# A two-layer graph attention kernel: one-hots and node loads moved to the end of a step, links ahead of most edge features, chunk 0 last in the sums, x read from the input

## The chip, the cores and the metric

The kernel runs on one core of a Trainium2 chip. The core has five engines that work side by side and wait for one another through semaphores: PE (TensorE, matmuls and transposes), DVE (VectorE), ACT (ScalarE), POOL (GpSimd) and SP (SyncE, which here only issues DMA transfers). The metric is the device time of one execution in microseconds (us); lower is better.

## The reference

A graph of N = 6250 nodes with D = 256 features and E = 200,000 edges, sorted by destination. The input is normalized, goes through two attention layers (4 heads of 64, then one head of 256), and is added back at the end. Cut to one layer:

```python
te = relu(edge_attr @ We + be) * exp(x @ Wo + bo)[src][:, None]        # 64 features of an edge
src, dst, ea = add_self_loops(src, dst, te, n)                         # a loop: mean of te over a node's edges
hx = (x @ Wg).reshape(n, heads, f)
he = (ea @ Wge).reshape(-1, heads, f)
al = leaky_relu((hx*a_s).sum(-1)[src] + (hx*a_d).sum(-1)[dst] + (he*a_e).sum(-1), 0.2)
al = exp(al - segment_max(al, dst)[dst])
al = al / segment_sum(al, dst)[dst]
out = segment_sum(hx[src] * al[:, :, None], dst) + b
x = relu(out + x)      # layer 0; layer 1: out + x + (the normalized input) + (the input)
```

So for every edge a row of its source node is fetched from a table, weighted by a softmax over the edges of its destination, and added up by destination.

## The kernel before

**Tables and steps.** The kernel first normalizes the nodes, multiplies them by the weights of layer 0 and writes table T0 to DRAM (this is the prologue). One row of T0 holds the 268 numbers that an edge needs (the 256 features of `hx`, and terms of the scores) and beside them, in the second half of a row of 2 x 268, a copy of x of that node. Since a gather sees the table as rows of 268, the source indices in `self.src` are doubled. T1, the table of layer 1, has the same two halves and is written during layer 0.

The 200,000 edges, padded, are 1563 chunks of 128 edges. A step handles 24 chunks (the last two of a layer 14 and 13), so that a layer has 66 steps; its destinations lie within a stretch of 112 nodes. In `edges()` one loop runs over the steps `st` of both layers, with work for the next step `nx` and the finished ones `pv` and `late` woven in. The order in which `edges()` calls its parts is the order on each engine's queue; nothing reorders it.

**A step, in the order of `edges()`:**
- `nodes` (SP): the node tile `tw` of a step two ahead, 112 rows of the table with x beside them, in one DMA. `load_lb`, `load_ea`, `load_fl` (SP): other inputs of later steps.
- `gather(nx)` (POOL, L846): 24 indirect DMAs, one for each chunk of 128 rows, into one of three G buffers. A batch can begin once the sums that read this buffer three steps earlier are complete.
- `logits(st)` (DVE, L1043 to L1060): scores of the edges and two scans for the maxima; `ends(st)` (PE, L1067): transposes what the scans leave at the edges of the chunks.
- `spread(nx)` (DVE, L964 and L965, in every second step, for two steps): one-hots of destinations that bring node terms to edges; `parts(nx)` (DVE L993 to L996, PE L1001): the node terms split into bf16 parts.
- `rphase1(nx)` (PE L935, ACT L940): edge features of the next step in two rounds, each of two halves of the columns (four matmul instructions) and one ReLU. It is a generator: `next(y)` runs one round and `drain(y)` the rest.
- `links(st)` (DVE scans L1077 and L1079, PE transpose L1084): maxima across chunk borders, with the previous step's last state.
- `rows2(late)` (PE L452, for the next layer's table), `maxima(st)` (DVE from L1094, ACT), `rphase2(nx)` (PE L949), `adst(nx)` (PE L1015), `scale(st)` (DVE L1148: one operation over all 24 chunks of G).
- `carried(st)` (DVE L1133 to L1138 in layer 0, L1130 and L1138 in layer 1): adds the previous step's unfinished last row into chunk 0 of G.
- `sums(st)` (PE L1160): the one-hot S of a chunk times its G, 48 matmul instructions for 24 chunks, all into one PSUM tile `u`.
- `edge_rows(nx)` (DVE L1029 and L1032), `onehots(nx)` (DVE L980), `finish(pv)` (outputs and rows of finished nodes), `evict(st)` (ACT L1165: `u` to U), `rows1(pv)` (PE L1253), `index_on` (DVE and others: the index work for later steps, in pieces).

`ending()` is a version of the same order for the last steps of a layer.

**The prologue** runs over groups of seven node tiles: statistics, normalization, transposes, matmuls, and `store(g)`, which writes a group's rows to T0. `keep_x(g)` copies x from an input `xt` to the second half of the rows of T0, from DRAM to DRAM (L350). Beside it runs `indices()`, which loads `src` (`self.src`) and doubles it in four operations of 392 columns (L478).

Where the order of the loop decides, these are the lines:

```python
self.gather(nx)
drain(self.logits(st))
self.ends(st)
self.spread(nx)
self.parts(nx)
y = self.rphase1(nx)
next(y)
self.links(st)
...
drain(self.scale(st))
self.carried(st)
self.sums(st)
```

Of the kernel before, what the change touches and what calls it, by code (L numbers as in the profile page):

```python
# [22 lines left out]
F32 = mybir.dt.float32  # L23
BF = mybir.dt.bfloat16
I32 = mybir.dt.int32
# [6 lines left out]
P = 128  # L32
# [47 lines left out]
class Kernel:  # L80
# [122 lines left out]
    def prologue(self):  # L203
# [7 lines left out]
        with ExitStack() as c:  # L211
# [33 lines left out]
            if NT * P < N + P:  # L245
                nc.sync.dma_start(self.T[0][NT * P:N + P, :], zero[:N + P - NT * P, :2 * L.TW])
            trows = [wp.tile([P, GT, L.TW], F32, name=f"trow{i}", bufs=1) for i in range(3)]
# [103 lines left out]

# [19 lines left out]
            for k in range(-3, len(tiles) + 1):  # L371
# [10 lines left out]
                if k == 5:  # L382
                    more()
                if k >= 8 and k % 4 == 0 and k // 4 - 2 < g0:
                    keep_x(k // 4 - 2)
                if 0 <= k + 1 < len(tiles):
# [71 lines left out]
    def indices(self, wp):  # L458
# [16 lines left out]
        yield  # L475
        for i in range(0, NCH, 392):
            src = self.src[:, i:min(NCH, i + 392)]
            V.tensor_scalar(src, src, 2.0, None, op0=OP.mult)  # L478
            yield
        scf = wp.tile([P, 11, NS], F32, name="scf", bufs=1)  # L480
# [168 lines left out]
    def edges(self, ctx):  # L649
# [30 lines left out]
        for k, st in enumerate(steps):  # L680
# [21 lines left out]
            next(y)  # L702
            self.links(st)
            if late:
                self.rows2(late)
# [10 lines left out]
            self.carried(st)  # L716
            self.sums(st)
            if late:
# [25 lines left out]
    def ending(self, st, nx, pv, late, after):  # L744
# [12 lines left out]
        y = self.rphase1(nx)  # L757
        next(y)
        self.links(st)
        if late:  # L760
# [20 lines left out]
        self.evict(st)  # L781
        y = self.rphase1(after) if after else iter(())
        next(y, None)
        drain(self.scale(nx, cuts=(1, 1 + c // 2, c)))
# [54 lines left out]
    def gather(self, st):  # L839
# [5 lines left out]
        for c in (range(0) if st["k"] == 0 and self.CX > last else (last, *range(last))):  # L845
            nc.gpsimd.indirect_dma_start(  # L846
                out=G[:, c, 0:L.TW], out_offset=None, in_=self.rows[L.l][0:2 * n, :],
                in_offset=bass.IndirectOffsetOnAxis(ap=idx[:, c:c + 1], axis=0))
# [56 lines left out]
    def nodes(self, st):  # L905
# [3 lines left out]
        st["tw"], st["xw"] = tw[:, :L.TW], tw[:, L.TW:L.TW + D]  # L909
        w = L.TW + D  # L910
        nc.sync.dma_start(tw[1:M + 1, :w], self.T[L.l][ds(r, M), 0:w])

    def halves(self, st):
# [5 lines left out]
    def rphase1(self, st):  # L919
# [11 lines left out]
        for i in range(2):  # L931
            r = slice(i * PH, (i + 1) * PH)
            y = self.ps_y.tile([P, 1024], F32, name="y")
            for w, o in self.halves(st):
                nc.tensor.matmul(y[:, o], self.webd[l][r, :], ea[r, w], start=True, stop=True)  # L935
            if c % 2:
                for w, o in self.halves(st):
# [125 lines left out]

    def ends(self, st):

        e = st["ends"]
# [256 lines left out]
    def general_layer(self, L, wp, pp):  # L1323
# [13 lines left out]
        with tc.For_i(0, self.NCH * P, P) as i:  # L1337
# [11 lines left out]
            old = wp.tile([P, L.W], F32, name=f"gold{l}")  # L1349
            sw, dw = [wp.tile([P, 1], I32, name=n) for n in ("gsi2", "gdi2")]  # L1350
            V.tensor_scalar(sw, si, 2.0, None, op0=OP.mult)
            V.tensor_scalar(dw, di, 2.0, None, op0=OP.mult)
            for t, tab, ix in ((G[:, :L.TW], self.rows[l], sw), (nd, self.rows[l], dw), (old, state, di)):
# [94 lines left out]
def layout(inputs):  # L1448
# [5 lines left out]
    a = {"x": np.concatenate([x, np.zeros((2 * P, D), np.float32)])}  # L1454
    a["xt"] = np.concatenate([a["x"], np.zeros((N + 2 * P, Layer(0).TW - D), np.float32)], 1)
    EP = NCH * P
# [63 lines left out]
```

## Time and profile before

| | us |
|---|---|
| median of 3 runs (lowest to highest) | 4721.76 (4721.40 to 4724.88) |
| the profiled execution | 4717.79 |
| its span | 4716.0 |
| busy: PE | 3204.3 (68%) |
| busy: POOL | 3015.5 (64%) |
| busy: DVE | 2842.0 (60%) |
| busy: ACT | 524.2 (11%) |
| first gather from T0 | 105.61 |

The profile shows one execution on the chip. In it a row of a group reads: line of the kernel, engine, operation, output<-inputs with their shapes, count | busy time and mean ns of one | idle time of the engine just before them, and what ended most of it. A row of the timeline reads: start, duration, engine, line, operation, and in brackets the idle time before it and what released it. "issue" is time in which the engine waited for nothing that the profile shows; "remote" is a release that it can't name by an instruction. A row of the windows gives busy time and instructions of each engine in a stretch of time, then the clock granted to PE, the DMA engines' mean busy share and GB/s. Shares over the whole span mix the prologue, two layers with different work and the passage between them, so a change in one stage is read from that stage.

### The profile page before, as it was taken

What the parts mean: (1) busy time and instruction counts of PE and PEld (TensorE: products, weight loads), DVE (VectorE), ACT (ScalarE), POOL (GpSimd) and SP (SyncE); (2) the same over time, 40 slices, a digit from 0 to 9 for tenths busy, and PEclk for the clock granted to TensorE, in tenths of its full rate; (3) what the DMA queues carried; (4) which work ended last, traced back from release to release, by engine and by line L of the source; (5) the groups of instructions that cost most, each with busy time, mean ns of one, the idle gap of its engine ahead of it and who ended that gap; (6) DMA issues with size and microseconds to landing.
All of it is one profiled execution on the core that took longest, in us unless ns stands there. A gap on an engine that the chain in (4) does not pass through costs nothing. (4 is left out here: it accounts for less than half of the span.)

```text
span 4716.0 us, 33666 instructions
## 1 busy us (share of the span) xinstructions
PE 3204.3 (68%) x9878; PEld 1931.3 (41%) x9878; DVE 2842.0 (60%) x6122; ACT 524.2 (11%) x1162; POOL 3015.5 (64%) x3255
## 2 busy tenths in 40 slices
PE   7677677776777777777755666666666666666666
PEld 5344444444444444444433334343433333343434
DVE  6566676666676666666664555555545555554546
ACT  4111111111111111111110000000000000000000
POOL 5566666666666666666636666666666666666664
PEclk8767767767777777676676777776777777776777
DMA  8344444444444444444434444444444444444442
GB/s 275 94 128 128 117 126 131 119 127 128 116 127 129 125 122 126 127 121 126 122 84 113 120 118 127 116 123 121 124 117 122 127 121 119 119 125 114 122 124 74
DMA packets 234171, 582.99 MB, mean 124 GB/s; under 512 B 62185, under 2 KB 84613, under 8 KB 233913
## 3 DMA queue, kind: packets, MB, share of 16 engines
q0 software_dynamic: 150144, 422.75, 34.1%
q1 hardware_dynamic: 83419, 157.36, 10.1%
q8 instruction: 79, 1.29, 0.1%
q14 instruction: 113, 0.93, 0.1%
q10 hardware_dynamic: 416, 0.67, 0.1%
HBM read 549.44 MB, written 37.92 MB: 125 GB/s over the span
## 5 line engine op out<-in xcount | busy, mean ns | idle before, releaser
L846 POOL DMA_INDIRECT G<-T,src x3102 | 2962.0, 955 | 1623.1 <-issue 898.9
L1160 PE MATMUL u<-G,S 128*128 128x270 f32 (+1 forms) x6252 | 1621.4, 411 | 750.2 <-issue 628.7
L1160 PEld LDWEIGHTS u<-G,S 128*128 128x128 f32 x6252 | 1235.8, 200 | 1075.8 <-issue 682.0
L935 PE MATMUL y<-ea,webd 64*128 64x384 f32 (+1 forms) x1056 | 734.8, 822 | 304.5 <-issue 269.2
L1148 DVE TENSOR_TENSOR G<-G,kps 128x6144 f32<-128x6144 f32 (+3 forms) x136 | 853.0, 6275 | 0.0
L1077 DVE TENSOR_TENSOR_SCAN cl<-fl,cl,lf 4x129 f32<-4x129 f32 (+1 forms) x130 | 61.2, 471 | 937.2 <-remote 657.0
L935 PEld LDWEIGHTS y<-ea,webd 64*128 64x128 f32 x1056 | 290.2, 298 | 597.1 <-issue 534.7
L949 PE MATMUL zad<-R,wea 128*64 128x384 f32 (+1 forms) x1056 | 464.3, 794 | 2.3 <-ACT R L940 1.0
L980 DVE TENSOR_TENSOR S<-kps,loc 128x3072 f32<-128x3072 f32 x132 | 437.6, 3315 | 4.5
L940 ACT ACTIVATE R<-y,webd 128x768 f32<-128x768 f32 x260 | 233.1, 897 | 627.6 <-PE y L935 272.3
L949 PEld LDWEIGHTS zad<-R,wea 128*64 128x64 f32 x1056 | 155.9, 202 | 314.1 <-issue 253.5
L1165 ACT ACTIVATE U<-u 128x270 f32<-128x270 f32 (+1 forms) x132 | 51.9, 393 | 1880.4 <-remote 913.1
L1029 DVE STREAM_TRANSPOSE rt<-zad 128x768 f32<-128x768 f32 (+1 forms) x130 | 124.5, 958 | 35.2 <-remote 27.8
L1067 PE MATMUL lf<-ident,fb 128*36 128x128 f32 (+1 forms) x132 | 47.1, 357 | 138.2 <-issue 108.7
L1001 PE MATMUL zad<-a,Q 128*128 128x12 bf16 (+1 forms) x132 | 24.4, 185 | 156.6 <-issue 98.5
L452 PE MATMUL fin<-wg,h1T 128*128 128x260 f32 x264 | 127.2, 632 | 1.8 <-ACT h1T L1255 1.8
L1094 DVE TENSOR_TENSOR fb<-flpen,lf 128x192 f32<-128x192 bf16 (+1 forms) x132 | 36.7, 278 | 148.2 <-PE lf L1084 128.6
L964 DVE TENSOR_TENSOR lb<-lb,kps 128x1536 bf16<-128x1536 bf16 (+1 forms) x68 | 113.0, 1661 | 0.0
L452 PE MATMUL ps<-wg,hT 128*128 128x266 f32 x292 | 89.9, 436 | 33.3 <-ACT hT L326 14.9
L452 PEld LDWEIGHTS fin<-wg,h1T 128*128 128x128 f32 x264 | 71.5, 299 | 48.5 <-issue 34.6
L1001 PEld LDWEIGHTS <-Q 128*128 128x128 bf16 x132 | 14.9, 113 | 180.2 <-issue 104.4
L1190 ACT ACTIVATE mw<-mw,mg 128x2 f32<-128x2 f32 x66 | 19.7, 298 | 608.0 <-DVE mg L1189 337.1
(191 smaller groups left out, 2079.4 us busy)
## 6 DMA issues: line engine op xcount, KB each, us to landing
G<-T,src POOLq DMA_INDIRECT x3102
ea<-in_ea_dram SPq DMA_DIRECT2D x64, 768.0 KB
lb<-locrow SPq DMA_DIRECT2D x64, 384.0 KB
tw<-T SPq DMA_DIRECT2D x66, 229.2 KB
T<-t1row SPq DMA_DIRECT2D x66, 227.5 KB
tw<-T SPq DMA_DIRECT2D x66, 225.8 KB
out_dram<-fb SPq DMA_DIRECT2D x64, 112.0 KB
T<-in_xt_dram SPq DMA_DIRECT2D x5, 938.0 KB
```

The lines of the kernel that those rows point to most:

```text
L452: self.nc.tensor.matmul(ps[:, :L.MW], hT[:, k, :], self.wg[L.l][:, k, :], start=(k == 0), stop=(k == 1))
L846: nc.gpsimd.indirect_dma_start(out=G[:, c, 0:L.TW], out_offset=None, in_=self.rows[L.l][0:2 * n, :], in_offset=bass.IndirectOffsetOnAxis(a ...
L935: nc.tensor.matmul(y[:, o], self.webd[l][r, :], ea[r, w], start=True, stop=True)
L940: nc.scalar.activation(R[:, i, :32 * c].rearrange("p (b n) -> p b n", b=2), y.rearrange("p (b n) -> p b n", b=2)[:, :, :16 * c], AF.Relu, ...
L949: nc.tensor.matmul(st["zad"][i * PH:(i + 1) * PH, o], self.wea[l][0], R[:, i, w], start=True, stop=False)
L964: V.tensor_tensor(lb[:, :, :n], lb[:, :, :n], self.k_part.unsqueeze(2).to_broadcast([P, i, n]), op=OP.is_equal)
L980: nc.vector.tensor_tensor(st["S"][:, c0:c1, :], self.k_iota.unsqueeze(1).to_broadcast(w), self.loc[:, o + c0:o + c1].unsqueeze(2).to_broad ...
L1029: V.transpose(rv[:, :32 * c].rearrange("p (b n) -> p b n", b=2), z.rearrange("p (b n) -> p b n", b=2)[:, :, :16 * c])
L1077: V.tensor_tensor_scan(cl[:H, :], fl[:H, :], lf[:H, 0:P + 1], init, op0=OP.add, op1=OP.max)
L1148: nc.vector.tensor_tensor(v, v, pw[:, c0:c1, :].unsqueeze(3) .to_broadcast([P, c1 - c0, H, L.F]), op=OP.mult)
L1160: nc.tensor.matmul(st["u"][:, :L.W], S[:, i, :], G[:, i, 0:L.W], start=(j == 0), stop=(j == c - 1))
L1165: self.nc.scalar.activation(U[:, :L.W], st["u"][:, :L.W], AF.Copy)
```

## The change

- Table T0 loses its second half: its rows are 268 wide, `keep_x` and the input `xt` are gone, and the gather of layer 0 uses rows without doubling. `store` writes whole rows.
- `self.src` is no longer doubled in the prologue, since layer 0 uses it as it is. Layer 1's table keeps two halves, so each step of layer 0 doubles its own 24 columns in `ends()`, after its gathers have used them.
- `nodes` of layer 0 loads `tw` in two DMAs: 112 x 268 from T0 and 112 x 256 from the input x. Layer 1 still uses one.
- `nodes` for three steps ahead stands at the end of a step. On SP's queue this is where the call at the head of the next step stood.
- `spread` for two steps ahead stands at the end of a step, after `index_on`: on DVE ahead of the next step's logits, and no longer behind them. The call `spread(nx)` in its old place then finds the work done.
- `rphase1` can pause after the first half of a round as well. With one `next(y)` before `links(st)` and one after, the transpose of the links (PE) stands after two of the eight L935 matmul instructions, and no longer after four.
- `sums` takes chunks 1 to 23 first and chunk 0, the only one that `carried` writes to, last.

```diff
-        self.T = [self.dp.tile([N + P, L.TW * 2], F32, name=f"T{L.l}") for L in self.L]
+        self.T = [self.dp.tile([N + P, L.TW * (1 + L.l)], F32, name=f"T{L.l}") for L in self.L]
...
-                nc.sync.dma_start(self.T[0][0:NT * P, :].rearrange("(p t) d -> p t d", p=P)
-                                  [:, ts[0]:ts[0] + n, 0:L.TW], trow[:, :n, :])
-
-            def keep_x(g):
-                ts, n = groups[g], len(groups[g])
-                to, of = (t.rearrange("(p t) d -> p t d", p=P)[:, ts[0]:ts[0] + n, :]
-                          for t in (self.T[0][0:NT * P, L.TW:2 * L.TW], a["xt"][0:NT * P, :]))
-                nc.sync.dma_start(to, of)
+                nc.sync.dma_start(self.T[0][0:NT * P, :].rearrange("(p t) d -> p t d", p=P)[:, ts[0]:ts[0] + n, :],
+                                  trow[:, :n, :])
...
-        for i in range(0, NCH, 392):
-            src = self.src[:, i:min(NCH, i + 392)]
-            V.tensor_scalar(src, src, 2.0, None, op0=OP.mult)
-            yield
...
             y = self.rphase1(nx)
             next(y)
             self.links(st)
+            next(y)
...
             self.carried(st)
-            self.sums(st)
+            self.sums(st, (1, st["C"]), (0, 1))
...
                 next(self.late, None)
+            for q in steps[k + 3:k + 4]:
+                if q["L"] is st["L"]:
+                    self.nodes(q)
+            for q in steps[k + 2:k + 3]:
+                if q["L"] is st["L"] and "lb" in q:
+                    self.spread(q)
...
-                out=G[:, c, 0:L.TW], out_offset=None, in_=self.rows[L.l][0:2 * n, :],
+                out=G[:, c, 0:L.TW], out_offset=None, in_=self.rows[L.l][0:n * (1 + L.l), :],
...
-        w = L.TW + D
+        w = L.TW + L.l * D
         nc.sync.dma_start(tw[1:M + 1, :w], self.T[L.l][ds(r, M), 0:w])
+        if L.l == 0:
+            nc.sync.dma_start(st["xw"][1:M + 1, :], self.a["x"][ds(r, M), :])
...
                 nc.tensor.matmul(y[:, o], self.webd[l][r, :], ea[r, w], start=True, stop=True)
+                if o.start == 0:
+                    yield
...
     def ends(self, st):
+        if st["L"].l == 0:
+            src = self.src[:, st["o"]:st["o"] + st["C"]]
+            self.nc.vector.tensor_scalar(src, src, 2.0, None, op0=OP.mult)
```

More of the change, by code (lines that the diff above doesn't have):

```diff
@@ L245, in prologue @@
             if NT * P < N + P:
-                nc.sync.dma_start(self.T[0][NT * P:N + P, :], zero[:N + P - NT * P, :2 * L.TW])
+                nc.sync.dma_start(self.T[0][NT * P:N + P, :], zero[:N + P - NT * P, :L.TW])
             trows = [wp.tile([P, GT, L.TW], F32, name=f"trow{i}", bufs=1) for i in range(3)]
@@ L383, in prologue @@
                     more()
-                if k >= 8 and k % 4 == 0 and k // 4 - 2 < g0:
-                    keep_x(k // 4 - 2)
                 if 0 <= k + 1 < len(tiles):
@@ L757, in ending @@
         y = self.rphase1(nx)
+        next(y)
         next(y)
@@ L782, in ending @@
         y = self.rphase1(after) if after else iter(())
+        next(y, None)
         next(y, None)
@@ L1349, in general_layer @@
             old = wp.tile([P, L.W], F32, name=f"gold{l}")
-            sw, dw = [wp.tile([P, 1], I32, name=n) for n in ("gsi2", "gdi2")]
-            V.tensor_scalar(sw, si, 2.0, None, op0=OP.mult)
-            V.tensor_scalar(dw, di, 2.0, None, op0=OP.mult)
+            sw, dw = [wp.tile([P, 1], I32, name=n) for n in ("gsi2", "gdi2")] if l else (si, di)
+            if l:
+                V.tensor_scalar(sw, si, 2.0, None, op0=OP.mult)
+                V.tensor_scalar(dw, di, 2.0, None, op0=OP.mult)
             for t, tab, ix in ((G[:, :L.TW], self.rows[l], sw), (nd, self.rows[l], dw), (old, state, di)):
@@ L1454, in layout @@
     a = {"x": np.concatenate([x, np.zeros((2 * P, D), np.float32)])}
-    a["xt"] = np.concatenate([a["x"], np.zeros((N + 2 * P, Layer(0).TW - D), np.float32)], 1)
     EP = NCH * P
```

## The prediction

> **What bounds the kernel now.** I read the page's costliest groups first, then busy time by windows around a step in the middle of each layer, then POOL and PE in order of time there, and the prologue last. The groups:
>
> ```profile
> span 4716.0 us, 33666 instructions
> L846 POOL DMA_INDIRECT G<-T,src x3102 | 2962.0, 955 | 1623.1 <-issue 898.9
> ```
>
> No engine is full, but POOL's 3102 gathers are busy 2962 us and idle 1623 us before them, together 4585 of the 4716 us. Inside a batch the idle time is issue (899 us, 0.30 us each); the rest lies between batches. Around one layer-0 step, in windows:
>
> ```profile
> 1218.00:1232.00 14.00, 13.03 (x28) 5.47 (x26) 11.39 (x18) 3.01 (x6) 10.40 (x11) 0.55 0.51 153
> 1232.00:1242.00 10.00, 9.38 (x40) 7.68 (x41) 8.91 (x24) 0.91 (x3) 7.58 (x8) 1.00 0.48 132
> 1242.00:1254.00 12.00, 3.98 (x9) 2.25 (x9) 4.75 (x13) 0.42 (x1) 4.99 (x6) 0.60 0.33 94
> ```
>
> (Columns: length, busy time and count of PE, weight loads, DVE, ACT, POOL; then granted clock, DMA share, GB/s.) A step has three thirds: a chain of edge features at half clock, sums at full clock, and 12 us in which PE and DVE do little. In order of time, POOL and PE:
>
> ```profile
> 1218.53 0.94 POOL L846 DMA_INDIRECT G<-T,src  x1 [5.89 <-PE u L1160]
> ...
> 1247.57 0.95 POOL L846 DMA_INDIRECT G<-T,src  x1 [0.30 <-issue]
> 1254.47 0.94 POOL L846 DMA_INDIRECT G<-T,src  x1 [5.95 <-PE u L1160]
> ...
> 1232.16 9.38 PE L1160 MATMUL u<-G,S 128*128 128x270 f32 x40 [0.83 <-issue]
> 1242.44 0.39 PE L1160 MATMUL u<-G,S 128*128 128x270 f32 x1 [0.90 <-issue]
> ...
> 1250.14 0.61 PE L1160 MATMUL u<-G,S 128*128 128x270 f32 x1 [1.49 <-issue]
> 1252.24 1.96 PE L1160 MATMUL u<-G,S 128*128 128x270 f32 x4 [1.49 <-issue]
> ```
>
> Twenty-four gathers take 1218.53 to 1248.52, 30.0 us. The next batch needs the G buffer that these sums read, so it waits for the last of the 48 matmuls and starts 35.94 us after the batch before. Forty matmuls take 9.4 us, but four single ones take the next 10 us ("issue": nothing the profile shows holds them). This stall lifts near 1252, some 3.7 us after the last gather, and four matmuls follow in 1.96 us, 0.49 us each. So a layer-0 step costs what the stall leaves of the sums. Layer 1:
>
> ```profile
> 3214.00:3228.00 14.00, 2.49 (x7) 1.40 (x7) 1.17 (x6) 0.00 (x0) 7.65 (x9) 0.61 0.36 102
> 3228.00:3239.00 11.00, 9.54 (x19) 3.56 (x18) 9.11 (x12) 2.39 (x4) 8.16 (x9) 0.56 0.34 90
> 3228.40 0.94 POOL L846 DMA_INDIRECT G<-T,src  x1 [4.31 <-remote]
> 3228.16 0.39 ACT L1165 ACTIVATE U<-u 128x261 f32<-128x261 f32 x1 [18.64 <-remote]
> ```
>
> Here the sums are nearly done when the stall comes, and POOL still restarts only when it lifts: a floor that does not move with the sums. Step lengths, from evictions of u (the first and last of 50 layer-0 steps, then of 58 layer-1 steps):
>
> ```profile
> 475.93 0.40 ACT L1165 ACTIVATE U<-u 128x270 f32<-128x270 f32 x1 [12.82 <-PE fin L1253]
> 2237.95 0.40 ACT L1165 ACTIVATE U<-u 128x270 f32<-128x270 f32 x1 [10.92 <-PE u L1160]
> 2612.48 0.39 ACT L1165 ACTIVATE U<-u 128x261 f32<-128x261 f32 x1 [18.61 <-PE zad L1001]
> 4597.30 0.39 ACT L1165 ACTIVATE U<-u 128x261 f32<-128x261 f32 x1 [18.64 <-remote]
> ```
>
> 1762.0/50 = 35.24 us in layer 0 and 1984.8/58 = 34.22 in layer 1. Layer 0 stands 1.0 us a step above the floor: that is all the steps can give, 62 us over its 61 or so full steps.
>
> **The change, part by part.**
>
> *Prologue: x no longer copied into table 0, indices no longer doubled there.*
>
> ```profile
> 40.00:60.00 20.00, 12.03 (x54) 9.50 (x55) 14.06 (x59) 7.56 (x20) 7.95 (x26) 0.83 1.06 330
> 60.00:80.00 20.00, 20.00 (x109) 16.66 (x108) 16.00 (x65) 16.18 (x43) 15.29 (x55) 1.00 1.06 310
> DMA packets 5969, 9.11 MB, mean 304 GB/s; under 512 B 783, under 2 KB 5132, under 8 KB 5900
> T<-in_xt_dram SPq DMA_DIRECT2D x5, 938.0 KB
> T<-in_xt_dram SPq DMA_DIRECT2D x2, 670.0 KB
> T<-in_xt_dram SPq DMA_DIRECT2D x2, 268.0 KB
> 45.19 0.36 DVE L478 TENSOR_SCALAR src<-src 128x392 int32<-128x392 int32 x1 [11.14 <-DMA src<-in_src_dram]
> ```
>
> Nine copies go, 5 x 938 + 2 x 670 + 2 x 268 = 6566 KB. Between 30 and 60 us the DMA engines move 304 GB/s, so this is 21.6 us of all of them. (The Trainium skill, "DMA: Bandwidth & Descriptors", section "Where 436 GB/s comes from", puts the engines' limit at 436 GB/s; by it the copies would be 15.1 us, an estimate; the trace's 304 decides here.) The doubling also loses DVE's 11.14 us wait, though the next index operations wait for a load of their own. Neither is gained whole: PE is full from 60 to 80, and idle 8 us from 40 to 60. I take 8 us; ends 0 (PE's work sets the end) and 20. The first steps' gathers then start earlier, into the stall already shown, which is why I stay low.
>
> *Doubling 24 chunks' indices at each layer-0 step*: one DVE operation more, queued ahead of the boundary transpose. The nearest row is a 128x24 operation (first below):
>
> ```profile
> 3231.28 0.18 DVE L1102 TENSOR_TENSOR mt<-al,m 128x24 f32<-128x24 f32 x1
> 104.89 2.15 SPq L911 DMA_DIRECT2D tw<-T  x3
> ```
>
> 0.2 us x 64 = 13 us at most; it usually falls into the stall, where DVE waits anyway: 0, ends 0 and +13. *Node tile in two DMAs*: SP spends 0.72 us on an issue (second row), 64 more. Behind it on SP's queue stand loads for later steps; the tile is asked for three steps ahead, some 105 us: 0. No row shows what one more issue does to the stall: −0 to +0.3 us a step by the 0.28 us that I find below for half a matmul left over; I take 0. POOL loses a DVE wait on the indices at no cost, since its first gather waits for PE.
>
> *Links after half of the first edge features, chunk 0 last* (layer 0):
>
> ```profile
> 1222.04 0.26 PE L1084 MATMUL lf<-ident,cl 36*128 36x36 f32 x1
> 1222.34 0.35 DVE L1094 TENSOR_TENSOR fb<-flpen,lf 128x192 f32<-128x192 bf16 x1 [1.79 <-PE lf L1084]
> 1224.58 6.54 DVE L1148 TENSOR_TENSOR G<-G,kps 128x6144 f32<-128x6144 f32 x1
> 1231.90 0.21 DVE L1138 SCALAR_TENSOR_TENSOR G<-U,slink,G 1x5 f32<-1x5 f32 x1
> 1230.83 0.50 PE L1015 MATMUL zad<-lb,aq 128*128 128x384 bf16 x2
> ```
>
> Two L935 matmuls, 0.73 us each by the 2.92 us for four (below, under layer 1), go behind the links transpose: it comes up to 1.4 us earlier, and so does the 6.54 us scaling. PE's own chain gets no shorter; its end at 1231.33 is what remains once chunk 0 no longer waits for the carried rows (to 1232.11). The sums start 0.8 us earlier. Whether the stall moves too isn't shown; if it stays, 0.8/0.23 = 3.5 matmuls more lie before it and 3.5 x 0.49 is over the whole 1.0; if it moves along, nothing is gained. I take 0.25 us x 46 steps = −11.5, ends 0 and −46.
>
> *One-hots of destinations at the end of a step.* The index work of every fourth step delays the logits, and with the two one-hot operations behind them the next step starts so:
>
> ```profile
> 1182.36 0.40 ACT L1165 ACTIVATE U<-u 128x270 f32<-128x270 f32 x1 [12.05 <-PE u L1160]
> 1182.79 1.73 DVE L964 TENSOR_TENSOR lb<-lb,kps 128x1536 bf16<-128x1536 bf16 x1
> 1185.66 0.19 PE L1001 MATMUL zad<-a,Q 128*128 128x12 bf16 x1 [2.33 <-DVE a L996]
> 1188.50 0.26 PE L1084 MATMUL lf<-ident,cl 36*128 36x36 f32 x1
> ```
>
> PE waits 2.33 us for parts that stand behind them on DVE, and the links come 6.1 us after the eviction. POOL's next batch starts at 1218.53, 36.17 us after this eviction; a batch follows its own eviction by 0.24 (3228.16 and 3228.40), so this step takes 35.9, 1.7 above the floor. With the pair ahead of the logits some of its 1.73 + 0.4 us falls into the stall; the logits are then late next, by no more than the pair. I take two thirds of the 1.7, −1.1 x 15 = −16.5; ends +5 (the logits late by 0.3) and −33 (the whole pair).
>
> *Layer 1.* The links wait for scans that the stall holds, and half of the edge features now stands behind that wait, at half clock:
>
> ```profile
> 3227.88 2.72 PE L935 MATMUL y<-ea,webd 64*128 64x384 f32 x4 [1.23 <-issue]
> 3231.65 2.92 PE L935 MATMUL y<-ea,webd 64*128 64x384 f32 x4 [0.99 <-ACT R L940]
> ```
>
> Here it costs PE up to 0.7 us; where all four ran in the stall, up to 1.4. The floor covers it: ACT waits 18.64 us for a u that is nearly complete when the stall begins, so the sums have several us of room. Without the cover it is 64 x 0.7 = 45 us. I take +1, ends −5 and +45. (The Trainium skill, "TensorE: Matmul & The Clock Gate", Part 1 on the clock gate, lets 3.4 us of work restore the clock, which would halve that price. The trace differs: from 1218 to 1232 PE is busy 13.03 of 14 us at 0.55.)
>
> **Sum.** −8 − 11.5 − 16.5 + 1 = −35. The profiled execution took 4717.79 us, which gives 4682.8; the median of the runs is 4.0 above it: 4687.
>
> **The rivals.**
> *A. Layer 0 falls to the floor.* For it: layer 1's steps and the shape of the stall, which ends with the gathers. Against: the stall is in every step and may come earlier with the work. 62 + 8 = −70: 4652.
> *B. The stall moves with the sums, and only the prologue counts.* For it: in layer 1, with sums that start earlier, the stall starts earlier too (near 3214, 14 us before the release, against 12 at 1242). −8 or nothing: 4714 to 4722.
> *C. Slower: the stall overtakes the sums of layer 0.* If it begins after so much work is issued, and the earlier links and doubled indices issue more before it, matmuls are left over at the release, each 0.49 us. From 0.27 matmuls a step (8/61/0.49) the prologue's gain is gone; at 1.5 it is 45 − 8 = +37: 4759. Against: layer 0's PE and DVE work per step hardly grows.
>
> **How the numbers follow.** 0.2% is 9.4 us, about what a measurement tells from no change. Forecast (4665 to 4712) 0.42, A 0.18, B 0.15, C 0.25. Faster is forecast and A, 0.60; same is B, 0.15; slower is C, 0.25. The range goes from A's 4645 to 4748, over half of C, and leaves out about 0.2.
>
> **What would show it.** Right: no copies into T from in_xt; the 60 to 80 us stretch without idle PE coming sooner, and the first table gather some 8 us sooner; layer-0 steps near 34.8; the links about 1.3 us sooner after the eviction in steps like 1218, and 2 us or more sooner in those like 1182; sums starting about 0.8 us sooner; layer 1 at 34.2. Wrong: a layer-0 step at or above 35.2 with more than four matmuls after the release (B, C), or layer-1 evictions more than 34.3 us apart.

## The result: 4756.72 us against 4722.64, and the profile after

| | before | after |
|---|---|---|
| median (lowest to highest), us | 4722.64 (4721.40 to 4726.35) | 4756.72 (4748.47 to 4759.31) |
| ratio of after to before | | 1.0067 (95% interval 1.0057 to 1.0077) |
| profiled execution's span, us | 4716.0 | 4755.3 |
| first eviction of u (prologue and first step), us | 192.4 | 179.3 |
| a step of layer 0, mean of 50, us | 35.24 | 35.82 |
| passage between the layers (eviction 60 to 66), us | 237.1 | 233.4 |
| a step of layer 1, mean of 58, us | 34.22 | 34.53 |

The change made the kernel 0.7% slower. The table adds up: the prologue gave 13.1 us, some 60 full steps of layer 0 took 0.58 x 60 = 35 more, the passage gave 4, and some 60 steps of layer 1 took 0.31 x 60 = 19 more: +37, against 39 between the spans. An execution more than 1.5% above the fastest of its kernel, which is taken to be in a slower state, is left out of every comparison; this concerns three of the four executions of run 10.

The page of the changed kernel has the same shape. POOL's gathers are busy 16 us less than before, and idle 65 us longer:

```profile
span 4755.3 us, 34012 instructions
L843 POOL DMA_INDIRECT G<-T,src x3102 | 2945.7, 950 | 1687.7 <-issue 904.9
```

The step lengths come from the same four evictions as before (the first and the last of 50 steps, then of 58):

```profile
467.90 0.40 ACT L1170 ACTIVATE U<-u 128x270 f32<-128x270 f32 x1 [10.69 <-PE u L1165]
2259.14 0.40 ACT L1170 ACTIVATE U<-u 128x270 f32<-128x270 f32 x1 [12.51 <-PE lf L1072]
2633.30 0.39 ACT L1170 ACTIVATE U<-u 128x261 f32<-128x261 f32 x1 [18.12 <-PE u L1165]
4636.24 0.39 ACT L1170 ACTIVATE U<-u 128x261 f32<-128x261 f32 x1 [17.86 <-PE u L1165]
```

The prologue did what was forecast, and more. In windows, and POOL's first gathers from the table:

```profile
40.00:60.00 20.00, 20.00 (x108) 16.39 (x107) 19.07 (x83) 15.94 (x40) 13.05 (x47) 1.00 0.90 327
60.00:80.00 20.00, 20.00 (x109) 16.75 (x108) 16.52 (x75) 15.72 (x42) 11.72 (x37) 1.00 0.75 217
89.78 0.94 POOL L843 DMA_INDIRECT G<-T,src  x1 [14.61 <-DMA T<-trow]
```

PE is busy from 40 us on, where it idled 8 of 20 us before, the DMA share falls from 1.06 to 0.75 in the second stretch, and the first gather starts at 89.78 instead of 105.61.

Now a layer-0 step, PE and POOL in order of time, that stands for most (36.1 us):

```profile
1257.31 0.94 POOL L843 DMA_INDIRECT G<-T,src  x1 [4.68 <-PE lf L1072]
1258.99 0.26 PE L1089 MATMUL lf<-ident,cl 36*128 36x36 f32 x1
1269.32 0.82 PE L1016 MATMUL zad<-lb,aq 128*128 128x384 bf16 x2
1269.93 9.43 PE L1165 MATMUL u<-G,S 128*128 128x270 f32 x39
1280.51 0.39 PE L1165 MATMUL u<-G,S 128*128 128x270 f32 x1 [1.14 <-issue]
1282.61 0.39 PE L1165 MATMUL u<-G,S 128*128 128x270 f32 x1 [1.72 <-issue]
1285.42 0.61 PE L1165 MATMUL u<-G,S 128*128 128x270 f32 x1 [2.42 <-issue]
1288.22 0.61 PE L1165 MATMUL u<-G,S 128*128 128x270 f32 x1 [2.19 <-issue]
1290.31 2.87 PE L1165 MATMUL u<-G,S 128*128 128x270 f32 x5 [1.48 <-issue]
1293.46 0.94 POOL L843 DMA_INDIRECT G<-T,src  x1 [6.46 <-PE u L1165]
```

The links come 1.7 us after the restart of POOL's batch (3.5 us in the step shown of before), the sums 12.6 us after it (13.6), with no wait for the carried rows. But the stall comes sooner too: its first single matmul is at 1280.5, 23.2 us after the restart, where it was 23.9. Thirty-nine matmuls lie before it instead of forty, and five follow the release instead of four. The means below take the stall to begin where PE first stands idle for more than 1 us behind the tenth matmul of the sums; the matmuls that it finds left are those of the 48 that start after that. Over layer 0's full steps in each trace, counted from the eviction, the sums start at 14.07 us before and 12.74 after, the stall begins at 24.8 and 23.0, and it finds 5.4 and 6.9 matmuls left.

Two kinds of steps lie under these means, and the clock granted to PE tells them apart. The step behind the one shown is of the other kind. First the windows at the head of the two steps (the granted clock is the third number from the end), then rows of PE in the second:

```profile
1257.00:1268.00 11.00, 10.57 (x21) 4.84 (x22) 9.32 (x13) 2.79 (x6) 8.25 (x9) 0.50 0.35 95
1293.20:1304.00 10.80, 7.97 (x28) 3.31 (x27) 9.74 (x12) 3.01 (x6) 8.10 (x9) 0.94 0.52 165
1296.87 1.55 PE L934 MATMUL y<-ea,webd 64*128 64x384 f32 x4
1303.98 12.44 PE L1165 MATMUL u<-G,S 128*128 128x270 f32 x46 [2.63 <-issue]
```

At a granted clock of 0.94 four edge-feature matmuls take 1.55 us, the sums start 10.8 us after the eviction, 46 of the 48 lie ahead of the stall, and the step takes 34.3 us. Every fourth step holds the index work. Of the 45 others, those whose first 10 us ran at 0.91 or more of the clock take 34.3 us in both kernels; there are 8 of them before and 14 after. The rest, at 0.50, take 34.96 us before and 35.91 after: their sums start 1.0 us sooner (12.49 instead of 13.46), but the stall begins 1.6 us sooner (22.11 instead of 23.75) and finds 8.0 matmuls left instead of 5.2.

In layer 1 the links wait for the stall's end, as forecast, and the cover was thinner than I took it to be. First the kernel before, at a step whose eviction is at 2680.7, then the changed kernel at one whose eviction is at 3356.89:

```profile
2672.79 0.80 PE L935 MATMUL y<-ea,webd 64*128 64x384 f32 x1 [2.32 <-issue]
2681.68 0.31 PE L1084 MATMUL lf<-ident,cl 33*128 33x33 f32 x1 [8.10 <-DVE cl L1079]
2690.52 1.81 PE L1160 MATMUL u<-G,S 128*128 128x261 f32 x7 [1.62 <-DVE G L1138]
```

```profile
3358.34 0.26 PE L1089 MATMUL lf<-ident,cl 33*128 33x33 f32 x1
3358.41 1.63 PE L934 MATMUL y<-ea,webd 64*128 64x384 f32 x2
3367.86 9.07 PE L1165 MATMUL u<-G,S 128*128 128x261 f32 x40 [0.20 <-DVE G L1153]
3378.89 0.38 PE L1165 MATMUL u<-G,S 128*128 128x261 f32 x1 [1.97 <-issue]
...
3390.78 1.47 PE L1165 MATMUL u<-G,S 128*128 128x261 f32 x3 [0.81 <-issue]
3392.29 0.39 ACT L1170 ACTIVATE U<-u 128x261 f32<-128x261 f32 x1 [18.13 <-PE u L1165]
```

Before, the whole first round of edge features (its last matmul is the first row) ran inside the stall of the step before, where PE had nothing else to do, and the sums began 9.8 us after the eviction. After, half of that round stands behind the links, outside the stall (second row); the sums begin 11.0 us after the eviction, eight of them meet the stall, three are still left at its end, and this step takes 35.40 us. It is one of 12 steps in 58 that take more than 35 us. In the kernel before, sums that start at 10.1 us, as they do in the mean, and take 10.8 us when nothing holds them (run 9) are done at 20.9, and the stall begins at 21.3: there was 0.4 us of room, and the links' new place takes 1.0. In the kernel before, 32 of the 58 steps left no matmul to the stall, in the changed kernel 2.

### The profile page after: what moved, and what is told of

It is laid out like the page before. It is cut to its first block, busy times and chain, and to the rows that moved or that the text cites. A ratio compares the mean times of both kernels' runs of the same rounds, so it can differ in the third digit from the quotient of the medians.

```text
span 4755.3 us, 34012 instructions
## 1 busy us (share of the span) xinstructions
PE 3246.0 (68%) x9878; PEld 1940.2 (41%) x9878; DVE 2850.4 (60%) x6184; ACT 512.9 (11%) x1162; POOL 2998.5 (63%) x3255
## 5 line engine op out<-in xcount | busy, mean ns | idle before, releaser
L1165 PE MATMUL u<-G,S 128*128 128x270 f32 (+1 forms) x6252 | 1705.4, 418 | 1068.1 <-issue 1028.3
L1165 PEld LDWEIGHTS u<-G,S 128*128 128x128 f32 x6252 | 1267.9, 205 | 1416.4 <-issue 1159.4
L934 PEld LDWEIGHTS y<-ea,webd 64*128 64x128 f32 x1056 | 275.9, 303 | 338.6 <-issue 206.9
L1122 DVE COPY G<-kps 128x96 f32<-128x96 f32 (+1 forms) x132 | 34.3, 260 | 131.9 <-ACT kps L1118 101.2
L1072 PEld LDWEIGHTS lf<-ident,fb 128*36 128x36 f32 (+1 forms) x132 | 18.3, 138 | 200.5 <-issue 114.0
L1252 DVE TENSOR_TENSOR t1row<-t1row,fb 128x256 f32<-128x256 f32 x66 | 28.1, 426 | 101.8 <-remote 58.8
L1258 PE MATMUL fin<-ident,fb 128*128 128x128 f32 x132 | 41.7, 396 | 64.5 <-issue 59.1
```

Source lines behind the costliest of these rows:

```text
L1072: self.nc.tensor.transpose(self.lf[0:e.shape[1], 1:P + 1], e, self.ident)
L1165: nc.tensor.matmul(st["u"][:, :L.W], S[:, i, :], G[:, i, 0:L.W], start=(j == 0), stop=(j == c - 1))
```

## The experiments

Each run is timed against the kernel before on the same chip, and the chips differ: the kernel before takes 4722 to 4726 us on the first chip and on that of the eighth to tenth run below, some 4776 us on those of the first to the seventh and of the eleventh to fourteenth, and 4084 us on that of the last two. So ratios are compared within a group of chips, and step lengths are given beside them. "The tables part" is the change without its order parts: x out of table 0, no doubling in the prologue, indices doubled in each step of layer 0, two node DMAs, with the call of `nodes` at the end of a step.

**1. The tables part alone.**

```diff
  (the changed kernel, without:)
-            next(y)                       # in rphase1's use, around links(st)
-            self.sums(st, (1, st["C"]), (0, 1))
+            self.sums(st)
-            for q in steps[k + 2:k + 3]:  # spread at the end of a step
-                ...
```

> Only the tables part of the change (table 0 without x, no doubling in the prologue, 24 indices doubled in each layer-0 step, two node DMAs); order of the step as before. Theory (the stall begins after a set amount of work is issued by PE, DVE and ACT: 191 instructions after the eviction in layer 0, 167 in layer 1, and the order parts of the change only move it): the prologue's 13 us and the passage's 4 are kept, and one more DVE instruction in a step costs 0 to 0.2 us a step: 4703 to 4718. Rival (the added DMA and its issue in each layer-0 step bring the stall earlier): layer 0 at 35.8 us a step, 4735 to 4745.

Measured: 4763.87 against 4775.5 us, ratio 0.9975 (0.9965 to 0.9986). The prologue's gain is kept (first eviction at 180.4 us), so the added DMA and the doubling cost little: a step of layer 0 takes 35.72 us, and 35.79 in the kernel before on a chip of this kind (run 7). The rival falls, on this kind of chip.

**2. The links' new place alone, on the kernel before.**

```diff
                 nc.tensor.matmul(y[:, o], self.webd[l][r, :], ea[r, w], start=True, stop=True)
+                if o.start == 0:
+                    yield
...
             self.links(st)
+            next(y)
```

> The kernel before with the links placed after half of the first edge features, nothing else. Theory: layer 0's stall comes earlier with its sums, no gain or up to +0.6 us a step; layer 1's sums start 0.7 to 1.1 us later and some steps end after the stall, +0.3 us a step; 4738 to 4775. Rival (the loss comes from the one-hots' or the sums' new place): layer 0 0.2 us a step faster, layer 1 unchanged, 4705 to 4722.

Measured: 4798.18 us, ratio 1.0056 (1.0037 to 1.0074), +23 us by the medians. The links' place costs time by itself. Here layer 0's steps take 35.98 (35.79 in run 7), layer 1's 34.76 (34.62).

**3. Eight small operations on ACT.**

```diff
             self.links(st)
+            for _ in range(8):
+                nc.scalar.activation(self.tiny, self.tiny, AF.Copy)
```

> The kernel before with eight one-column ACT copies more in each step, behind the links, on an engine that is 11% busy; nothing waits for them. Theory: they use up 8 of the 191 (167) instructions, the stall begins about 1 us earlier, and in layer 0 about 3 more matmuls are left to it: +0.5 to +1.1 us a step, 4752 to 4790, with the count before the stall (all engines but POOL and SP) unchanged. Rival (the stall is set by time or by the gathers, whatever the other engines issue): 4719 to 4730.

Measured: 4790.25 us, ratio 1.0030 (1.0018 to 1.0041). Neither theory meets it. The count before the stall did not stay: with ACT's in it, it rose from 161 (run 7) to 174 in layer 1. There the stall began 2.3 us later (23.8 us after the eviction) and found 0.7 matmuls left instead of 4.3, and the steps even got shorter (34.40 against 34.62). Layer 0's steps took 36.26 (35.79). So in layer 1 ACT's instructions do not bring the stall sooner; that they stand ahead of the second ReLU on ACT's queue can explain layer 0's loss, but wasn't tried by itself.

**4. One-hots back behind the logits, the rest as changed.**

```diff
-            for q in steps[k + 2:k + 3]:
-                if q["L"] is st["L"] and "lb" in q:
-                    self.spread(q)
```

> The changed kernel with the one-hots of destinations back behind the logits. Theory: they are two instructions wherever they stand, so the time stays within 8 us of the changed kernel, 4748 to 4765. Rival (the one-hots ahead of the logits delay the logits in the stall and are the cause): 4700 to 4725.

Measured: 4791.23 us, ratio 1.0029 (1.0017 to 1.0041). As a ratio this lies between the ranges of the theory and of the rival. The kernel is still slower than the one before, so the one-hots' new place isn't the cause of the loss. The whole change comes out 0.25% faster in run 7, but on another chip, so what the one-hots' place is worth isn't shown.

**5. Links back, the rest as changed.**

```diff
-                if o.start == 0:
-                    yield
...
             self.links(st)
-            next(y)
```

> The changed kernel with the links back behind the whole first round of edge features; table, one-hots and sums as changed. Theory (the links' new place is the cause, since a stall that follows the sums by some 10 us takes what an earlier start gives, and more): faster than the kernel before by the tables' part, ratio 0.996 to 0.999, layer 0 about 0.5 us a step below the changed kernel. Rival (the one-hots ahead of the logits cost as much): ratio 1.001 to 1.006.

Measured: 4764.38 against 4776.73 us, ratio 0.9978 (0.9967 to 0.9988): as fast as the tables part alone. So without the links' new place the change is a gain, but not by the order: layer 0's steps take 35.92 us, although the sums start at 12.8 us in a step instead of 14.0 (run 7). The theory said 0.5 us a step below the changed kernel; that is missed, run 7 has 35.91. In layer 1, on the same chip, the steps take 34.66 us here and 34.86 in the changed kernel: the links' new place costs 0.2 us there.

**6. The tables part, in layer 0 the links behind both rounds.**

```diff
             next(y)
+            if st["L"].l == 0:
+                drain(y)
             self.links(st)
```

> The tables part alone, and in layer 0 the links placed behind both rounds of edge features (1.4 us of PE work later than before); layer 1 as before. Theory (the stall follows the sums, and the work issued before it grows with time): a later start costs little, the stall comes 1 to 1.5 us later, layer 0 within 0.3 us a step of the tables part alone, or faster by up to 0.5; ratio 0.990 to 1.001. Rival (the start of the sums sets the step, so 1.4 us later is 1.4 us longer less the room): layer 0 +0.7 to +1.4 us a step, ratio 1.006 to 1.016.

Measured: 4829.40 us, ratio 1.0104 (1.0087 to 1.0121); layer 0's steps take 36.80 us, 1.0 more than in the kernel before on this chip (run 7). That is in the rival's range. But the links come 1.0 us later and the sums 3.5 us (17.6 us after the eviction instead of 14.0), and the stall begins 4.8 us later (29.4 instead of 24.6), as the theory has it. So a later start costs less than it is late, and an earlier one (run 5) gains nothing.

**7. The changed kernel and the kernel before, on the chip of runs 5 and 6.**

> The changed kernel again, on the chip of the runs beside it: ratio 1.004 to 1.009 if its loss is the same from chip to chip.

> The kernel before, profiled on the chip of the runs beside it: the ratio is 1; the steps of layers 0 and 1 show where this chip differs, 35.2 and 34.2 us if it is like the first chip, some 0.4 us more each if it is like the second.

Measured: the changed kernel 4780.94 us, ratio 1.0004 (0.9994 to 1.0013); the kernel before, one run, 4780.11. On this chip the loss is gone, but the steps are longer here too. The first eviction comes 17 us sooner than in the kernel before (182.4 against 199.3) and the passage gives 2; the steps take back some 22: 35.91 and 34.86 us in the changed kernel, 35.79 and 34.62 in the kernel before. So layer 1 loses 0.24 us a step, nearly as on the first chip (0.31), and layer 0 only 0.12 instead of 0.58. Layer 0's steps at half clock got longer on this chip as well (36.60 against 35.66, the index steps left out), but 27 of 45 ran at full clock instead of 11. Why the kernel before has longer steps here than on the first chip isn't shown; its sums of layer 1 begin 11.24 us after the eviction instead of 10.14, and it leaves 4.3 matmuls to the stall where it left 0.9.

**8. A small operation of POOL behind each gather, on the tables part.**

```diff
                 in_offset=bass.IndirectOffsetOnAxis(ap=idx[:, c:c + 1], axis=0))
+            nc.gpsimd.memset(self.tiny, 0.0)
```

> The tables part alone, with one 128x1 memset on POOL behind each gather (0.09 us each by POOL's rows), so that a batch takes 32.3 instead of 30.0 us. Theory (the stall comes from gathers following one another, and the step is set by what it leaves of the sums): the stall begins later or is shorter; layer 1, whose floor was 34.2 to 34.6 us, changes by no more than 0.5 us a step; layer 0 loses up to 0.5. Rival (POOL's batch and a fixed gap of 4 us set the floor): 2.2 us a step more, 36.4 in layer 1, ratio 1.05 and over.

Measured: 4775.47 against 4725.71 us, ratio 1.0107 (1.0090 to 1.0124). The edit did not do what it was for: from first to last gather a batch still took 28.9 us in layer 1, as in the kernel before, the memset having gone into the 0.30 us between gathers. Steps of 35.82 and 34.66 us are those of the tables part in run 1 (35.72, 34.66), but that was a chip on which the kernel before is 1% slower. So either the memsets cost time, or the tables part is itself slower than the kernel before on a chip of this kind, which is the first chip's. It was not timed alone on one, and this stays open; it is a rival for the loss in layer 0.

**9. Half the gathers.** Every second chunk's rows are zeros instead of table rows, except the last chunk's, so the result leaves out nearly half the edges' source rows. A step keeps 13 gathers, and POOL writes the zeros of the 11 other chunks between them.

```diff
+            if st["k"] > 2 and c % 2 and c != last:
+                nc.gpsimd.memset(G[:, c, 0:L.TW], 0.0)
+                continue
             nc.gpsimd.indirect_dma_start(
```

> The tables part alone with every second chunk's rows not gathered: POOL writes zeros there (so the result is not the reference's). Theory: with 12 gathers in a step there is no stall, all 48 matmuls run at full pace, and a step is PE's and DVE's work alone, 24 to 27 us. Rival (the stall comes from the work of PE, DVE and ACT itself): single matmuls more than 1 us apart remain at the end of the sums, and a step stays over 30 us.

Measured: 3438.3 us (one run), steps of 26.5 and 23.0 us. The sums of a layer-1 step, and their group in the page:

```profile
2003.53 10.83 PE L1160 MATMUL u<-G,S 128*128 128x261 f32 x48 [1.59 <-DVE G L1138]
L1160 PE MATMUL u<-G,S 128*128 128x270 f32 (+1 forms) x6252 | 1626.6, 425 | 335.4 <-DVE G L1138 333.3
```

All 48 matmuls stand in one row of 10.83 us, and of the group's 335.4 us of idle time 333.3 are waits for DVE. With 13 gathers in a step and writes between them there is no stall. It belongs to the gathers, not to PE's and DVE's work alone; whether to their number or to their pace, this run can't tell.

**10. Eight small matmuls on PE, on the tables part.**

```diff
             self.rphase2(nx)
+            for _ in range(8):
+                nc.tensor.matmul(self.lf[0:1, 500:501], self.ident[:, 0:1], self.ident[:, 0:1], start=True, stop=True)
             self.adst(nx)
```

> The tables part alone with eight 128x1x1 matmuls more on PE in each step, between the edge features' second product and the adding of node terms (0.5 to 0.8 us of PE). Theory (the stall begins after a set number of instructions): 16 records more before it, the stall finds 3 to 4 more matmuls left, layer 0 +0.6 to +1.5 us a step, ratio 1.006 to 1.018. Rival (the number of instructions does not matter, the sums only start 0.5 to 0.8 us later): layer 0 and 1 within 0.4 us a step, ratio 0.998 to 1.005.

Measured: 5099.55 us (one execution) against 4725.71, 7.9% more. That is 374 us, or 2.8 us for each of 132 steps, for eight calls with one column of output each (16 matmul and 16 weight-load records). The profile is of an execution that is left out, so no step lengths are given. It is more than either theory asked for and speaks against the rival; that the added instructions bring the stall sooner isn't shown by it.

**11. Eight small operations on DVE, on the tables part.**

```diff
+            for _ in range(8):
+                nc.vector.tensor_copy(self.tiny, self.ones)
             self.sums(st)
```

> The tables part alone with eight 128x1 copies more on DVE in each step, behind the carried rows (some 0.6 us of DVE beside the sums; nothing waits for them). Theory, as it now stands (PE and DVE together issue 157 to 162 instructions from an eviction to the stall in layer 1, some 175 in layer 0; ACT and POOL do not count): the sum stays at 157 to 162 in layer 1 and PE's share of it falls by about 8, so four more matmuls are left to the stall; +0.5 to +1.6 us a step, ratio 1.003 to 1.018. Rival (PE alone counts): PE's count before the stall stays at 120 to 123 in layer 1, steps within 0.2 us, ratio 0.997 to 1.001.

Measured: 4864.08 against 4777.27 us, ratio 1.0168 (1.0147 to 1.0189); steps of 36.95 and 34.98 us, 1.2 and 0.3 more than the tables part; in layer 0 the links come 1.5 us later for them (5.4 us after the eviction against 3.9). In time, DVE's instructions count, as the theory said. In the count they do not: of the 159 instructions before the stall in layer 1, PE's share is 122, and it was 123 of 156 with the tables part. That it would stay was the rival's sign.

**12. Small operations moved from DVE to ACT and POOL, on the tables part.**

```diff
-        V.tensor_copy(G[:, :c, L.p:L.p + H].rearrange("p c h -> p h c"),
+        nc.scalar.activation(G[:, :c, L.p:L.p + H].rearrange("p c h -> p h c"),
...
-            self.nc.vector.tensor_scalar(src, src, 2.0, None, op0=OP.mult)
+            self.nc.gpsimd.tensor_scalar(src, src, 2.0, None, op0=OP.mult)
```

> The tables part alone with small operations taken off DVE: the copy of the weights into G and the copy of a step's last destination go to ACT, the doubling of the indices to POOL; two to three DVE instructions fewer in a step. Theory: two to three of the counted instructions fewer, 0.1 to 0.2 us each in layer 0 and less in layer 1: 0.2 to 0.5 us a step, ratio 0.990 to 0.996. Rival (no count): 0.996 to 1.000, or slower where PE waits for ACT's copy.

Measured: 4815.13 us, ratio 1.0076 (1.0058 to 1.0093), a miss. The edit brought a new wait, to be read at POOL's first gather of a layer-1 batch, beside the eviction ahead of it:

```profile
2691.36 0.39 ACT L1162 ACTIVATE U<-u 128x261 f32<-128x261 f32 x1 [18.16 <-remote]
2692.18 0.94 POOL L837 DMA_INDIRECT G<-T,src  x1 [5.45 <-ACT U L1162]
```

ACT now writes into G, so a gather into G waits for ACT, and ACT's last work there is the eviction: POOL restarts 0.8 us behind it instead of 0.24. Steps take 36.16 and 35.06 us, 0.4 more than the tables part in both layers, about what the wait adds; so the run tells nothing on the count.

**13. Edge features behind the ReLU in bf16, on the tables part.**

```diff
-        st["R"] = R = self.wp.tile([P, 2, 32 * C], F32, name="R", bufs=1)
+        st["R"] = R = self.wp.tile([P, 2, 32 * C], BF, name="R", bufs=1)
...
-            wea = cp.tile([P, PH], F32, name=f"wea{L.l}")
+            wea = cp.tile([P, PH], BF, name=f"wea{L.l}")
```

> The tables part alone with the edge features behind the ReLU, and the weights that they meet in the second product, in bf16: four matmuls and four weight loads fewer on PE in each step, and some 1.5 us less PE work. Theory: 8 of the counted instructions fewer, the stall finds some four matmuls fewer: layer 0 near its floor, 34.3 to 35.0 us a step, layer 1 34.2 to 34.4; ratio 0.980 to 0.990. Rival (order and start set the step): the sums start up to 1.5 us sooner and the stall with them, ratio 0.993 to 0.999.

Measured: 4713.92 against 4777.27 us, ratio 0.9860 (0.9841 to 0.9879), the fastest against the kernel before, and faster than the changed kernel as well. Eight records fewer on PE in a step; layer 0's steps take 35.21 us (35.72), layer 1's 34.35 (34.66). Layer 0 stays above the range that I gave. The stall begins 2.9 us later in layer 0 and 1.8 in layer 1, and finds 3.4 and 0.0 matmuls left instead of 6.1 and 4.9; in layer 0 the sums start 0.5 us later than with the tables part, so an earlier start is not what gains there. The edit takes away PE time as well as instructions, and which of the two it was isn't shown.

**14. Both.**

> The two together, 10 to 11 counted instructions fewer in a step. Theory: both layers at the floor of 34.2 us, ratio 0.978 to 0.987. Rival: 0.990 to 0.999.

Measured: 4786.38 us, ratio 1.0016 (1.0006 to 1.0025), outside both ranges: the wait of run 12 takes back what run 13 gave.

**15. The changed kernel in bf16, and the same with the links back.** The edit of run 13 on the changed kernel, and on run 5's.

> The changed kernel with the edge features behind the ReLU and their weights in bf16, as in the run with that edit on the tables part alone (ratio 0.986). Theory (with the same instructions, another order only moves the slow stretch): no better than there, ratio 0.984 to 0.992. Rival (the order pays once fewer matmuls are left to the slow stretch): ratio 0.972 to 0.982, layer 0 below 34.7 us a step.

> The same without the links' new place: table, one-hots and sums as changed, edge features in bf16. Theory: 0.983 to 0.988, 0 to 0.4% below the run beside it, since layer 1 keeps four L935 matmuls ahead of the links. Rival: slower than the run beside it by 0.5% or more.

Measured: 4070.59 and 4072.05 us, against 4083.64 for the kernel before on that chip: ratios 0.9966 (0.9954 to 0.9979) and 0.9971 (0.9961 to 0.9982). Both miss the ranges, which were made for another chip. On this one there is next to no stall, and POOL never rests (the page of the first of the two, and its first and last of 58 layer-1 evictions):

```profile
L843 POOL DMA_INDIRECT G<-T,src x3102 | 2952.2, 952 | 1006.8 <-issue 937.3
2190.96 0.39 ACT L1170 ACTIVATE U<-u 128x261 f32<-128x261 f32 x1 [6.38 <-PE u L1165]
3938.73 0.39 ACT L1170 ACTIVATE U<-u 128x261 f32<-128x261 f32 x1 [6.16 <-PE u L1165]
```

1747.8/58 = 30.13 us a step, which is 24 gathers of 0.95 + 0.30 us. All of POOL's idle time but 69 us is issue. Here neither the links' place nor the matmuls saved can count; the 12 to 13 us gained are as much as the prologue's part gave elsewhere (13.1 us on the first chip), though the kernel before was not profiled on this chip.

## Why the prediction was wrong

I forecast 4687 us and a gain; it was a loss of 34 us. Point by point, on the chip of the prediction:

- **What bounds the kernel** was read rightly: POOL's batch, and a stall at its end that sets when the next batch can begin. Run 9 shows that the stall goes when nearly half the gathers go, run 15 that without it a step is POOL's 30.1 us.
- **Prologue: −8 taken, −13 measured.** Right in kind, under-sized. PE's idle time between 40 and 60 us went as a whole.
- **Doubling in the steps, two node DMAs: 0 taken.** Runs 1 and 7 bear it out within 0.1 us a step, on chips where the kernel before takes 4776 us; for the kind of the first chip run 8 leaves it open. (The 0.28 us for half a matmul is worked out nowhere in the prediction; half of 0.49 is 0.25.)
- **Links after half, chunk 0 last, layer 0: −11.5 taken for 46 steps.** This is the step that failed. The mechanics came as told (links 1.2 to 2.2 us sooner, sums not waiting for the carried rows), and I wrote that nothing is gained if the stall moves along; but I then took a gain of a quarter of a microsecond, with no gain as the worst end. The stall moved by more than the sums did: at half clock 1.6 us against 1.0, with 8.0 matmuls left to it instead of 5.2, and these steps took 0.95 us more. As 14 of the 45 ran at full clock instead of 8, the 45 got 0.56 us longer in the mean, +25. On the chip of runs 5 and 7 the changed kernel lost 0.1 us a step in layer 0, with the links' new place and without it (35.91 and 35.92 to 35.79). So on the first chip the step is known and its cause is not: neither the order parts nor the tables part was timed alone on a chip of that kind.
- **One-hots: −16.5 taken for 15 steps.** The steps concerned went from 36.5 to 37.25 us, +11. The links did come sooner (6.5 to 4.3 us after the eviction) and the sums as well (16.6 to 15.1), with the same end: the stall came at 24.1 instead of 26.5 and found 10.2 matmuls left instead of 8.0. The row-reading was right and its worth was not.
- **Layer 1: +1 taken, +19 measured**, inside the ends of −5 and +45. The price of 0.7 to 1.4 us on PE was right, and "several us of room" was wrong: there was 0.4 us. The first round ran inside the stall in most steps of the kernel before, for nothing, and half of it outside afterwards. Runs 5 and 7, on one chip, show the links' place as the cause (34.66 and 34.86 us a step).
- **Rival C** came within 3 us of the time, with a chance of 0.25. It had the sign of layer 0 (1.5 matmuls more left to the stall, as measured, at 0.49 us each) but put 45 us there, where 36 came, missed layer 1's 19, and took 8 for the prologue's 13. That these errors nearly cancel is luck.

The account behind it is in part argued: PE and DVE slow down after some amount of work, so an earlier start brings the slow stretch earlier. For it: in layer 0 the stall begins between 22.8 us (run 4) and 29.4 us (run 6) after the eviction, while the instructions that PE (with its weight loads) and DVE have issued by then stay at 170 to 176 (means of the layer's steps in each trace, run 10 left out). Against it: step by step the count isn't fixed, 163 to 186 in the changed kernel's layer 0. And in layer 1 it is 152 to 161, but there the time is as steady, 20.9 to 21.7 us (23.2 to 23.8 in runs 3, 13 and 14), so layer 1 can't tell the two apart. Runs 10 and 11 show that more instructions lengthen the steps, run 13 that fewer, with less PE time, shorten them, run 5 that an earlier start alone gains nothing. What I could not settle is what the stall is. It needs the gathers (run 9), and ACT's instructions do not bring it sooner (run 3, layer 1). The engines' own instruction fetches, which the trace lists as DMA packets of the kind "instruction", are not in most of the stalls: in the kernel before, one falls between 2 us ahead of the stall and the next eviction in 19 of 50 steps of layer 0 and 15 of 58 of layer 1. And the chip of run 15 hardly shows it. The packets of the gathers took as long there as on the first chip (0.173 us in the mean, taken between 1000 and 2000 us), so the transfers themselves are not slower where it is seen.

The Trainium skill, "TensorE: Matmul & The Clock Gate", Part 1 on the clock gate, says that some 3.4 us of work restore the clock. The changed kernel's windows around the step above differ from it, and bear out the price that I took instead:

```profile
1257.00:1270.00 13.00, 12.57 (x25) 5.49 (x26) 11.18 (x18) 2.86 (x7) 9.64 (x11) 0.50 0.36 98
1270.00:1279.00 9.00, 9.00 (x40) 7.45 (x39) 7.84 (x20) 0.83 (x3) 6.87 (x8) 0.96 0.50 136
```

PE is busy 12.57 of 13 us at half clock, and at full clock only in the sums. In those 13 us it runs mostly matmuls on 64 rows or columns (64*128, 128*64). Their size alone is not the reason: in the step behind, the same matmuls run at 0.94. The price was too simple there: it holds for steps that begin at half clock.

## What to carry to other kernels

When an engine slows down at a point that moves with the work issued before it, moving work forward may only move that point; try taking work away (run 13), and price an instruction by what an added one costs in a run, not by its own duration. Before taking a mean over steps, sort them by the clock granted at their head: here a fifth to a third of the ordinary steps ran at full clock, and had no loss. Work that runs inside a stall is free, so see what a reordering takes out of it before counting what it brings forward. And where a kernel waits for something that no row names, time it on more than one chip before believing half a per cent.

## What the runs showed of the hardware

Three things were unexpected. The same kernel takes 4722, 4776 or 4084 us depending on the chip, with repeats on one chip within 0.5%, and on the chip of the 4084 us the changed kernel in bf16 runs without the stall. Eight one-column fp32 matmul calls in a step cost 2.8 us a step in the mean (run 10, one execution). And a wait added to POOL's first gather (run 12) costs 0.4 us a step although the operation waited for, an eviction of 0.39 us, follows at once on what POOL waited for before.
